# Column tiles 20 to 29 of double blocks 2 to 4: two heads' weights summed over tile pairs, one weight of eight made on ScalarE and GpSimd

## The chip, the cores and the metric

The kernel runs on one core of a Trainium2 chip. The core has five engines that work side by side, each through its own queue in order: TensorE (matmuls; PE in the profile), VectorE (DVE), ScalarE (ACT), GpSimd (POOL) and SyncE (SP, which here only issues DMAs). They wait for one another on semaphores. The metric is the time on the device in microseconds (us). Before the change it is 1262.46 us, the median of three runs (1262.27 to 1264.15).

## The reference

A graph attention layer over 4096 nodes with 256 features and 4 heads, and then a mixture of 8 experts of which each node uses 2:

```python
h = jnp.einsum('nd,hdk->hnk', x, W)                  # x normalised first
s_col = jnp.einsum('hnk,hk->hn', h, a1)
s_row = jnp.einsum('hnk,hk->hn', h, a2)
e = leaky_relu(s_row[:, :, None] + s_col[:, None, :], negative_slope=0.2)
e = jnp.where(adj[None, :, :] > 0, e, NEG_INF)
att = softmax(e, axis=-1)
h_prime = jnp.einsum('hij,hjk->hik', att, h)
y = elu(out) + x @ Wr + br
return gamma * (y - mu) / jnp.sqrt(var + LN_EPS) + beta
...
for e in range(E):                                   # weights w_dense: softmax over the best two
    h = gelu(xf @ W1[e] + b1[e])
    out = out + w_dense[:, e:e + 1] * (h @ W2[e] + b2[e])
```

Both layers are added to their input. The whole 4096 x 4096 attention matrix of each head has to be formed, masked by `adj`, summed and multiplied by `h`.

## The kernel before

**The attention.** The rows (destinations) are worked on in 4 double blocks of 1024 (`a` = 0 to 3 in the code, two halves of 512 each; the text calls them double blocks 1 to 4), and for each of them the kernel walks over 32 column tiles of 128 sources (`j`). The exponential of a leaky relu of a sum is a maximum of two products; factors of a row or of a column alone are taken out of it. What is left is, for each head, `max(er, eb)` with `er` from the row and `eb` from the column, and the mask, which is 0 or 2, takes the rest by a minimum. So one VectorE instruction makes the weights of a head for 128 sources and 1024 rows (`weigh`, L1689, in the order of heads 1, 0, 2, 3). The column's other factor is already in `ha` (the features of the sources) and in `unit` (the same factor, for the sums).

For one tile TensorE then does two things (`attend`, L1212). `rows_of_head` (L1194, matmul L1198) adds weights times features into four accumulator banks `acc`, 16 matmuls; a matmul writes 32 of the array's 128 columns, so that four stand side by side. `weights_of_head` (L1204, matmul L1207) adds weights times `unit` into the bank `den`, from which the sums of the softmax come: 8 matmuls, each with 2 columns that are used. In `den` each head has one quarter, and the halves are its two rows. `queue` (L529) chains every matmul of the loop to the one before it: TensorE's order is the order of the program. In the first and last tile of a double block the sums are done first.

**The masks.** SP loads 512 KB of `adj` for a tile (`load_mask`, L1597), ScalarE turns it into a bfloat16 mask `am` (L1606). There are three buffers of each, and ten of a head's weights (`w`), so VectorE can run at most two and a half tiles ahead of TensorE.

**Finishing a double block.** `finish_blocks` (L1393) is a Python generator: while the loop goes over the next double block, each tile lets it go on by one step (`next(pending, None)`). It divides by the sums, adds the residual, normalises, and then `route_rows` (L1243) chooses the two experts of each row. Its steps at tiles 17 and 18 transpose the rows on TensorE into two banks each (L1253), which ScalarE copies out (L1256); at tile 19 the router's logits take two banks (L1264, copied at L1269), at tiles 20 and 24 one bank each (L1273, L1325). In the end GpSimd writes the rows into the experts' lists with 16 indirect DMAs (L1385), about from tile 25 on.

**PSUM.** There are 8 banks: four are `acc`, one is `den`, and three rotate under the tag "bank" (`bank`, L245) for everything else.

**The order of the other engines.** It isn't written out. The program is handed to a planner, which fixes the order of each engine's queue when the kernel is built: it goes through the work as it becomes ready by its own clock, takes what stands first in the program where several things are ready, and gives a buffer of a tag out when its first instruction is placed. On the chip that order is then kept, whatever comes late.

**Around it.** In double block 4 SP loads the first rows and weights for the experts (`first_tile`, L1580) at tile 3, and TensorE turns those rows after tile 29 (`turn_first`). After it comes the expert phase: 27 jobs of up to 512 rows of one expert, products L1872 and L1906, whose results GpSimd adds into the output (L1931), while the last double block is finished alongside.

Of the kernel before, what the change touches and what calls it, by code (L numbers as in the profile page):

```python
# [18 lines left out]
P = 128  # L19
# [14 lines left out]
LIST = 36 * CH  # L34
PLACE = (2, 3, 0, 1)
ORDER = (1, 0, 2, 3)

# [7 lines left out]
def gat_then_moe(  # L45
# [173 lines left out]
    def forward(apart, stack):  # L219
# [16 lines left out]
        def first_large(name):  # L236
            return fin.tile([P, TB, D], F32, tag="first", name=name, bufs=2)
# [377 lines left out]
        with ExitStack() as layer:  # L615
# [588 lines left out]
            def weights_of_head(w, j, half, h):  # L1204
# [5 lines left out]
                ))  # L1210

            def attend(w, j, halves, sums_first=None):  # L1212

# [21 lines left out]

            def shares_of(pd):

                z = small.tile([P, TB, H, HB], F32, tag="z", name="z")
                for h in range(0, H, 2):
                    nc.vector.reciprocal(z[:, :, h : h + 2], pd[:, :, PLACE[h] : PLACE[h] + 2, :HB])  # L1240
                return z

            def route_rows(b, xe):  # L1243
# [102 lines left out]
                if b == 0:  # L1346
# [34 lines left out]
                    nc.vector.tensor_tensor(others, others, least, OP.max)  # L1381

                for t in range(n):
                    for k in range(2):
# [8 lines left out]
            def finish_blocks(a):  # L1393
# [16 lines left out]
                z = shares_of(pd)  # L1410
                xe = rows_listed()
# [110 lines left out]
            def turn_sums(ud):  # L1522
                pd = bank([P, TB, H, Q], "pd")
                for t in range(TB):
                    queue(nc.tensor.transpose(
                        pd[:, t].rearrange("p h q -> p (h q)"), ud[:, ts(t, P)], ident
                    ))
                z = shares_of(pd)
                return z

# [148 lines left out]
            else:  # L1679

                with tc.tile_pool(name="sep", bufs=2) as work:

                    def weigh(er, am, j, halves):
# [11 lines left out]
                        return w  # L1695

                    both = list(range(HB))
                    ers = [er0, er1]
# [410 lines left out]
```

## Time and profile before

| | |
|---|---|
| time, median of 3 runs | 1262.46 us (1262.27 to 1264.15) |
| the profiled execution | 1260.56 us, span 1258.8 us |
| TensorE's granted clock | 0.999 |
| TensorE busy | 1241.7 us |
| VectorE busy | 845.5 us, of which weights (L1689) 605.9 us, 1275 ns each |
| ScalarE busy | 448.3 us, of which masks (L1606) 130.6 us, 1054 ns each |
| GpSimd busy | 240.4 us |
| matmuls of the attention | L1198 672.1 us in 4096 records, L1207 469.2 us in 2048 |
| double block 3: first matmul of tile 20, of tile 30 | 540.1 us, 592.5 us |

The span runs from the first to the last instruction of the program; the time of an execution has about 2 us around it. Busy times of matmuls overlap, because the ends of pipelined matmuls are modelled: steps from start to start are what counts. In a line of groups stand line, engine, operation, `out<-in`, shape and count, then busy us and mean ns, then the idle time of the engine just before, with what ended it. In a timeline the columns are start, duration, engine, line, operation, and in brackets how long the engine had been idle and what released it.

### The profile page before, as it was taken

What the parts mean: (1) busy time and instruction counts of PE and PEld (TensorE: products, weight loads), DVE (VectorE), ACT (ScalarE), POOL (GpSimd) and SP (SyncE); (2) the same over time, 40 slices, a digit from 0 to 9 for tenths busy, and PEclk for the clock granted to TensorE, in tenths of its full rate; (3) what the DMA queues carried; (4) which work ended last, traced back from release to release, by engine and by line L of the source; (5) the groups of instructions that cost most, each with busy time, mean ns of one, the idle gap of its engine ahead of it and who ended that gap; (6) DMA issues with size and microseconds to landing.
All of it is one profiled execution on the core that took longest, in us unless ns stands there. A gap on an engine that the chain in (4) does not pass through costs nothing.

```text
span 1258.8 us, 22720 instructions
## 1 busy us (share of the span) xinstructions
PE 1241.7 (99%) x8872; PEld 650.4 (52%) x8872; DVE 845.5 (67%) x1566; ACT 448.3 (36%) x918; POOL 240.4 (19%) x217
## 2 busy tenths in 40 slices
PE   9999999999999999999999999999999999999997
PEld 5444444332233332333325324888888876666686
DVE  7998887879999999999999995855111111111120
ACT  4332322265522365322655221533332332222322
POOL 4000000001002601006110024125322222122222
PEclk9999999999999999999999999999999999999999
DMA  6334433536533646334375422868998895455662
GB/s 215 118 118 126 155 107 102 166 104 145 177 114 103 225 112 201 116 94 158 107 178 183 133 70 77 276 171 219 259 236 239 227 219 116 102 139 105 140 160 37
DMA packets 155541, 190.23 MB, mean 151 GB/s; under 512 B 72312, under 2 KB 125680, under 8 KB 155040
## 3 DMA queue, kind: packets, MB, share of 16 engines
q1 hardware_dynamic: 133392, 145.39, 39.7%
q0 software_dynamic: 20544, 36.74, 13.2%
q10 hardware_dynamic: 1488, 6.55, 1.4%
q8 instruction: 71, 1.16, 0.4%
q14 instruction: 46, 0.38, 0.1%
HBM read 155.77 MB, written 29.74 MB: 147 GB/s over the span
## 4 chain that ended last, share of the span: by engine, by line
PE 93%; DVE 3%; issue 1%; ACT 1%; DMA 1%; POOLq 0%; SPq 0%; DVEq 0%; ACTq 0%
PE acc L1198 33%; PE po L1906 18%; PE ph L1872 17%; PE den L1207 17%; PE pr L1053 2%; DVE w L1689 2%; PE ph L1101 2%; PE ptx L1253 0%; DMA early<-lists 0%; PE acc L894 0%; PE pt L780 0%; PE ptr L1491 0%; PE po L1945 0%; PE pl L1264 0%; PE po L875 0%
## 5 line engine op out<-in xcount | busy, mean ns | idle before, releaser
L1198 PE MATMUL acc<-w,ha 128*32 128x512 f32 x4096 | 672.1, 593 | 2.3 <-ACT u L1401 0.9
L1689 DVE SCALAR_TENSOR_TENSOR w<-er,eb,am 128x1024 f32<-128x1024 f32 x496 | 605.9, 1275 | 36.2 <-PE den L1207 30.3
L1207 PE MATMUL den<-w,unit 128*2 128x512 f32 x2048 | 469.2, 592 | 0.4 <-issue 0.3
L1198 PEld LDWEIGHTS acc<-w,ha 128*32 128x32 f32 x4096 | 186.7, 110 | 293.7 <-issue 254.3
L1606 ACT ACTIVATE am<-adj 128x1024 bf16<-128x1024 int32 x124 | 130.6, 1054 | 347.8 <-DVE w L1689 213.1
L1872 PE MATMUL ph<-xT,w 128*128 128x256 f32 (+5 forms) x864 | 230.2, 424 | 2.1 <-issue 1.9
L1906 PE MATMUL po<-w,hT 128*128 128x256 f32 (+1 forms) x1040 | 229.7, 379 | 0.0
L1876 ACT ACTIVATE hT<-ph,bias 128x256 f32<-128x256 f32 (+5 forms) x216 | 111.1, 517 | 290.2 <-issue 185.8
L1906 PEld LDWEIGHTS po<-w,hT 128*128 128x128 f32 (+1 forms) x1040 | 195.7, 189 | 31.2 <-issue 3.1
L1919 DVE SCALAR_TENSOR_TENSOR o<-po,share,b2s 128x256 f32<-128x256 f32 (+2 forms) x66 | 31.7, 482 | 250.2 <-PE po L1906 211.4
L1872 PEld LDWEIGHTS ph<-xT,w 128*128 128x128 f32 x864 | 163.4, 190 | 62.0 <-issue 40.3
L1207 PEld LDWEIGHTS den<-w,unit 128*2 128x2 f32 x2048 | 94.7, 85 | 148.5 <-issue 140.0
L1931 POOL DMA_INDIRECT out<-o,ids x66 | 102.0, 1546 | 321.9 <-DMA out<-o,ids 136.4
L1385 POOL DMA_INDIRECT lists<-xe,at x64 | 88.3, 1379 | 267.6 <-issue 184.7
L1856 DVE STREAM_TRANSPOSE xT<-xr 128x512 f32<-128x512 f32 (+5 forms) x21 | 17.8, 850 | 34.0 <-PE ph L1872 31.2
L1053 PE MATMUL pr<-wr,xT 128*128 128x256 f32 x128 | 30.4, 381 | 0.2 <-ACT er L1147 0.2
L1894 ACT ACTIVATE b2s<-b2b,share 128x256 f32<-128x256 f32 x68 | 30.1, 499 | 0.0
L1121 POOL DMA_DIRECT2D residual<-rb x6 | 4.7, 784 | 121.2 <-DVE rb L1068 121.2
L1441 POOL DMA_DIRECT2D xf<-in_x x6 | 8.1, 1351 | 102.2 <-ACT xf L1440 102.2
L1053 PEld LDWEIGHTS pr<-wr,xT 128*128 128x128 f32 x128 | 24.1, 190 | 5.4 <-issue 0.9
L1101 PE MATMUL ph<-wall,xT 128*128 128x264 f32 x96 | 24.6, 399 | 0.0
L207 ACT ACTIVATE m<-y,off 128x256 f32<-128x256 f32 x48 | 23.7, 495 | 1.1 <-DVE off L215 0.6
(394 smaller groups left out, 618.8 us busy)
## 6 DMA issues: line engine op xcount, KB each, us to landing
adj<-in_adj SPq DMA_DIRECT2D x126, 512.0 KB
w<-in_L_ffn_W SPq DMA_DIRECT2D x54, 1024.0 KB
er<-parts ACTq DMA_DIRECT2D x3, 2048.0 KB
lists<-zeros POOLq DMA_DIRECT2D x8, 520.0 KB
residual<-rb POOLq DMA_DIRECT2D x8, 512.0 KB
rb<-residual SPq DMA_DIRECT2D x8, 512.0 KB
out<-y POOLq DMA_DIRECT2D x8, 512.0 KB
xb<-in_x SPq DMA_DIRECT2D x7, 512.0 KB
```

The lines of the kernel that those rows point to most:

```text
L1053: order_of(nc.tensor.matmul(pr[:, k, :], turned[b][:, c, ts(t0 + k, P)], wr[:, c, :], start=(c == 0), stop=(c == DC - 1),))
L1101: order_of(nc.tensor.matmul(phs[t - t0], xT[:, c, ts(t, P)], wall[:, c, :], start=(c == 0), stop=(c == DC - 1),))
L1198: queue(nc.tensor.matmul(acc[half][h // 2][here : here + Q, :], ha[:, j, h * K + g * Q : h * K + (g + 1) * Q], w[half][h], start=(j == 0), ...
L1207: queue(nc.tensor.matmul(den[here : here + HB, :], unit[:, j, h, 1 - half : 1 - half + HB], w[half][h], start=(j == 0 and half == 0), stop ...
L1385: ins = nc.gpsimd.indirect_dma_start(lists, bass.IndirectOffsetOnAxis(ap=at[:, k, t : t + 1], axis=0), xe[:, t, :], None,).ins
L1606: nc.scalar.activation(am, at, AF.Relu, scale=2.0)
L1689: marks["w"] = nc.vector.scalar_tensor_tensor(wh[:, these], er[:, these, h], eb[:, j, h : h + 1], mask[:, these], op0=OP.max, op1=OP.min,).ins
L1872: order_of(nc.tensor.matmul(ph, job["w1"][:, c, ts(f, P)], xT[:, c, :], start=(c == 0), stop=(c == DC - 1),))
L1876: job["gelu"] = nc.scalar.activation(hT[:, f, :], ph, AF.Gelu, bias=job["bias"][:, f : f + 1]).ins
L1906: order_of(nc.tensor.matmul(po[:size], hT[:, f, k * CH : k * CH + size], w2[:, f, :], start=(f == 0), stop=(f == FC - 1),))
L1919: given_out.append(nc.vector.scalar_tensor_tensor(o[:size], po[:size], share[:size, k : k + 1], b2s[k][:size], op0=OP.mult, op1=OP.add,).ins)
L1931: added.append(add().ins)
```

## The change

It concerns double blocks 2 to 4. In their tiles 20 to 29 (five pairs of an even and an odd tile):

- The sums of heads 1 and 0 are no longer added tile by tile. ScalarE scales the even tile's weights of such a head by the ratio of the two tiles' factors (`ratio`), GpSimd adds the odd tile's weights, and one set of matmuls over the sum serves both tiles (`added_pair`). The ratios are computed at the start of double block 2.
- In the odd tile the weights of head 3 are made without VectorE: ScalarE turns the mask into 0 or 1 (sign), and makes the maximum as a relu of a difference and an addition; GpSimd multiplies by the mask.
- The mask that VectorE reads in these tiles lies in PSUM: ScalarE copies it there, two bfloat16 values as one integer (`packed_mask`). Two tiles of the tag "bank" hold it, taken at tile 20.

In all tiles of double blocks 2 to 4 the quarters of `den` are assigned by head parity and half instead of by head, the matmuls of the sums stand in another order, and the shares are read accordingly. The step of `finish_blocks` that writes the lists waits for tile 30.

```diff
+PAIRED = (20, 30)
+ADDED = (1, 0)
+APART = 3
...
+            def place_of(h, half):
+                return 2 * (h % 2) + half
+            def weights_by_half(w, j, half, h, start=False, stop=False):
+                here = place_of(h, half) * Q
+                queue(nc.tensor.matmul(
+                    den[here : here + HB, :], unit[:, j, h, 1 - h // 2 : 1 - h // 2 + HB],
+                    w[half][h], start=start, stop=stop,
+                ))
+            def attend_both(w, j, alone, summed=None, sums_first=False):
+                halves = range(HB)
+                def first_heads():
+                    for half in halves:
+                        for h in (1, 0):
+                            rows_of_head(w, j, half, h)
+                def other_heads():
+                    if alone:
+                        for h in (1, 0):
+                            for half in halves:
+                                weights_by_half(w, j, half, h, start=(j == 0))
+                    for half in halves:
+                        for h in (2, 3):
+                            rows_of_head(w, j, half, h)
+                    for h in (2, 3):
+                        for half in halves:
+                            weights_by_half(
+                                w, j, half, h, start=(j == 0 and not alone), stop=(j == NT - 1)
+                            )
+                    if summed:
+                        for h in ADDED:
+                            for half in halves:
+                                weights_by_half(summed, j, half, h)
+                parts = (first_heads, other_heads)
+                for add in reversed(parts) if sums_first else parts:
+                    add()
...
+                if not ordered[0]:
+                    yield "lists"
                 for t in range(n):
                     for k in range(2):
                         ins = nc.gpsimd.indirect_dma_start(
...
+                    def packed_mask(am, j):
+                        pm = masks[j % 2]
+                        nc.scalar.copy(pm.bitcast(I32), am.bitcast(I32))
+                        return pm.bitcast(BF16)
+                    def weigh_both(er, a, j):
+                        am = load_mask(a, j)
+                        mask = packed_mask(am, j) if paired(j) else am
+                        w = [[None] * H for half in range(HB)]
+                        for h in ORDER:
+                            wh = work.tile([P, HB, B], F32, tag="w", name="w", bufs=10)
+                            if paired(j) and j % 2 and h == APART:
+                                nc.scalar.sign(am, am)
+                                nc.scalar.activation(
+                                    wh, er[:, :, h], AF.Relu, bias=less[:, j // 2 : j // 2 + 1]
+                                )
+                                nc.scalar.activation(
+                                    wh, wh, AF.Identity, bias=eb[:, j, h : h + 1]
+                                )
+                                nc.gpsimd.tensor_tensor(
+                                    wh, wh, am.rearrange("p (s r) -> p s r", s=HB), OP.mult
+                                )
+                            else:
+                                marks["w"] = nc.vector.scalar_tensor_tensor(
+                                    wh, er[:, :, h], eb[:, j, h : h + 1],
+                                    mask.rearrange("p (s r) -> p s r", s=HB),
+                                    op0=OP.max, op1=OP.min,
+                                ).ins
+                            made[j % 2][h] = wh
...
+                    def added_pair(j):
+                        w = [[None] * H for half in range(HB)]
+                        for h in ADDED:
+                            s = first_large("s").rearrange("p t d -> p (t d)")
+                            s = s.rearrange("p (s r) -> p s r", s=HB)
+                            nc.scalar.activation(
+                                s, made[0][h], AF.Copy, scale=ratio[:, j // 2, h : h + 1]
+                            )
+                            nc.gpsimd.tensor_tensor(s, s, made[1][h], OP.add)
...
                     for a in range(NR):
-                        later = None
+                        later, step = None, None
+                        if a == 1:
...
+                            nc.vector.tensor_scalar(ratio, pairs[:, :, 1], TINY, None, op0=OP.max)
+                            nc.vector.reciprocal(ratio, ratio)
+                            nc.vector.tensor_tensor(ratio, ratio, pairs[:, :, 0], OP.mult)
+                            nc.vector.tensor_scalar(ratio, ratio, 1.0 / EPS, None, op0=OP.min)
...
+                            nc.vector.tensor_scalar(less, alone[:, :, 1], -1.0, None, op0=OP.mult)
                         for j in range(0 if a else TB, NT):
-                            attend(
-                                weigh(er, load_mask(a, j), j, both), j, both,
-                                False if (a, j) == (NR - 1, NT - 1) else None,
-                            )
+                            if a == 0:
+                                attend(weigh(er, load_mask(a, j), j, both), j, both)
+                            else:
+                                if j == PAIRED[0]:
+                                    masks = [bank([P, B], "pm") for k in range(2)]
+                                w = weigh_both(er, a, j)
+                                attend_both(
+                                    w, j, not paired(j),
+                                    added_pair(j) if paired(j) and j % 2 else None,
+                                    j == 0 or j == NT - 1 and a + 1 < NR,
+                                )
                             if a == 0:
                                 prepare_at(TB + j)
-                            if pending:
-                                next(pending, None)
+                            if pending and (step != "lists" or j >= PAIRED[1]):
+                                step = next(pending, None)
```

More of the change, by code (lines that the diff above doesn't have):

```diff
@@ L1234, in attend, with shares_of @@
                     add()
-            def shares_of(pd):
+            def shares_of(pd, by_half):
                 z = small.tile([P, TB, H, HB], F32, tag="z", name="z")
+                if by_half:
+                    for k in range(0, H, 2):
+                        nc.vector.reciprocal(
+                            z[:, :, k : k + 2].rearrange("p t h s -> p t (h s)"), pd[:, :, :, k // 2]
+                        )
+                    return z
                 for h in range(0, H, 2):
@@ L1409, in finish_blocks @@
                     ))
-                z = shares_of(pd)
+                z = shares_of(pd, apart and a > 0)
                 xe = rows_listed()
@@ L1527, in turn_sums @@
                     ))
-                z = shares_of(pd)
-                return z
+                return shares_of(pd, apart)
             def last_block(b, u, z, given, xe):
@@ L1695, in weigh, with paired @@
                         return w
+                    def paired(j):
+                        return PAIRED[0] <= j < PAIRED[1]
+                    def packed_mask(am, j):
[26 more added lines that the diff above has]
+                            made[j % 2][h] = wh
+                            for half in range(HB):
+                                w[half][h] = wh[:, half]
+                        return w
@@ new lines, in added_pair @@
+                    def added_pair(j):
[7 more added lines that the diff above has]
+                            nc.gpsimd.tensor_tensor(s, s, made[1][h], OP.add)
+                            for half in range(HB):
+                                w[half][h] = s[:, half]
+                        return w
@@ L1697, in forward @@
+                    made = [[None] * H for k in range(2)]
+                    ratio = gat.tile([P, NT // 2, 2], F32)
+                    less = gat.tile([P, NT // 2], F32)
                     both = list(range(HB))
@@ L1729, in forward @@
                     for a in range(NR):
[L1730 to L1735 removed]
+                        later, step = None, None
+                        if a == 1:
+                            pairs = unit[:, :, :2, 1].rearrange("p (n k) h -> p n k h", k=2)
+                            nc.vector.tensor_scalar(ratio, pairs[:, :, 1], TINY, None, op0=OP.max)
+                            nc.vector.reciprocal(ratio, ratio)
+                            nc.vector.tensor_tensor(ratio, ratio, pairs[:, :, 0], OP.mult)
+                            nc.vector.tensor_scalar(ratio, ratio, 1.0 / EPS, None, op0=OP.min)
+                            alone = eb[:, :, APART].rearrange("p (n k) -> p n k", k=2)
+                            nc.vector.tensor_scalar(less, alone[:, :, 1], -1.0, None, op0=OP.mult)
+                        for j in range(0 if a else TB, NT):
+                            if a == 0:
[8 more added lines that the diff above has]
+                                    j == 0 or j == NT - 1 and a + 1 < NR,
+                                )
                             if a == 0:
                                 prepare_at(TB + j)
[L1738 to L1739 removed]
+                            if pending and (step != "lists" or j >= PAIRED[1]):
+                                step = next(pending, None)
                             if a == 1 and j == 1:
```

## The prediction

> **What bounds the kernel now.** I read the page's busy line and its chain first, then the timeline of the tiles that the change touches, engine by engine.
>
> ```profile
> PE 1241.7 (99%) x8872; PEld 650.4 (52%) x8872; DVE 845.5 (67%) x1566; ACT 448.3 (36%) x918; POOL 240.4 (19%) x217
> PE 93%; DVE 3%; issue 1%; ACT 1%; DMA 1%; POOLq 0%; SPq 0%; DVEq 0%; ACTq 0%
> 367.30:418.90 51.60, 51.60 (x501) 15.40 (x493) 50.46 (x71) 12.39 (x14) 16.83 (x10) 1.00 0.38 116
> 540.10:591.60 51.50, 51.50 (x491) 15.08 (x483) 49.36 (x64) 12.38 (x14) 16.51 (x11) 1.00 0.40 123
> ```
>
> TensorE is the end of the chain. The last two lines are the windows of tiles 20 to 29 in double blocks 2 and 3 (PE, weight load, DVE, ACT, POOL busy): TensorE is never idle, VectorE nearly full, ScalarE has 12 us of 51, GpSimd 17, all of it list writes.
>
> TensorE's timeline gives the step, VectorE's the rate of the weights:
>
> ```profile
> 353.88 1.09 PE L1253 MATMUL ptx<-ident,xe 128*128 128x128 f32 x8
> 354.90 1.92 PE L1198 MATMUL acc<-w,ha 128*32 128x512 f32 x16
> 356.64 0.60 PE L1207 MATMUL den<-w,unit 128*2 128x512 f32 x2
> 356.66 0.60 PE L1198 MATMUL acc<-w,ha 128*32 128x512 f32 x2
> 357.07 0.60 PE L1207 MATMUL den<-w,unit 128*2 128x512 f32 x2
> 355.43 13.24 DVE L1689 SCALAR_TENSOR_TENSOR w<-er,eb,am 128x1024 f32<-128x1024 f32 x11
> ```
>
> Four recorded matmuls, one for each quarter of the array's columns, start together every 0.43 us. A program matmul is recorded twice (4096 for 2048 in L1198), so four program matmuls cost 0.858 us, and a tile of 24 costs 5.15 us. VectorE makes a weight every 13.24 / 11 = 1.204 us, 4.82 us a tile. It leads, but gains only 0.33 us a tile.
>
> ScalarE's timeline shows what I take to decide the case:
>
> ```profile
> 353.20 1.06 ACT L1606 ACTIVATE am<-adj 128x1024 bf16<-128x1024 int32 x1 [3.73 <-DVE w L1689]
> 357.98 1.06 ACT L1606 ACTIVATE am<-adj 128x1024 bf16<-128x1024 int32 x1 [3.73 <-DVE w L1689]
> 358.94 1.05 ACT L1256 COPY xT<-ptx 128x512 f32<-128x512 f32 x2
> ```
>
> The masks at 353.20 and 357.98 belong to tiles 21 and 22 (counted through L1606). The copies behind them empty the banks that TensorE filled at 353.88, after tile 17: they stand in ScalarE's fixed order behind the mask of tile 22, which waits for VectorE to free a mask buffer, so they come 4 us late. Today this is free: there are three rotating banks and TensorE takes the next.
>
> **What the skill says.** The Trainium skill, "SBUF — State Buffer", Who interferes with whom: a VectorE instruction with two SBUF inputs contends with GpSimd reading SBUF, one with at most one SBUF input outside the 2-port modes does not. GpSimd's timeline agrees with the first half: list writes take 2.08 us while weights are made and 0.97 us once VectorE has stopped. No run here shows the second half.
>
> ```profile
> 751.81 2.08 POOL L1385 DMA_INDIRECT lists<-xe,at  x1 [0.30 <-issue]
> 766.85 0.97 POOL L1385 DMA_INDIRECT lists<-xe,at  x1 [0.30 <-issue]
> ```
>
> "TensorEngine Tiling (Array Packing)", Key Properties: column tiles work independently; the fourfold starts above agree. "PSUM — Partial Sum Buffer", Specifications: a bank holds 512 FP32 values of a partition, so each packed mask fills one.
>
> **The change, part by part.**
>
> *Removed from TensorE.* A pair of tiles has 16 den matmuls. The 8 of heads 1 and 0 become 4 on the summed weights: 4 fewer, 0.858 us. Fifteen pairs (5 in each of 3 double blocks): **-12.87 us**. A pair then takes 10.30 - 0.86 = 9.44 us.
>
> *New order of matmuls, all 96 tiles.* Every four still cover four column quarters, but twice a tile the order within a four turns from quarters 2, 3, 0, 1 to 0, 1, 2, 3 or back. Starts within a four lie about 7 ns apart, so a turn costs 0 to 14 ns: 0 to 2.7 us. I take 0.5.
>
> *VectorE.* Seven weights a pair instead of eight: 7 x 1.204 = 8.43 us, under 9.44. A PSUM input may add some[...]. At worst 7 x 1.28 = 9.0, still under. The set-up at block 2 is five small operations of some 0.16 us (the L177 row, 158 ns), 0.8 us, hidden by VectorE's lead; uncovered, 0.8.
>
> *ScalarE.* Added in a pair: two packs of 512 (L1256's 580 ns), a sign (L1606's 1054), then Relu, Identity and two scaled copies at 1054 plus some 0.09 for a per-partition operand (L1481's 589 against L207's 495): 1.16 + 1.05 + 4 x 1.14 = 6.8 us, and two masks, 2.1: 8.9 us, less about 0.1 overlap per instruction, about 8. Fits 9.44 with little room. Cover gone, it costs its excess over 9.44.
>
> *GpSimd.* A product and two sums of 1024. No such row before: the skill, "GPSIMD Engine Reference", Performance versus the Vector engine, has 4497 ns for 2048, so an estimate of 2.3 us each, 6.9 us a pair, below 9.44. At the port-blocked end (plus 1.2 each) 10.5: over by 1.1 a pair, 16 us in all. The masks in PSUM are there against that, so I take 2.3. The last pair's sums run beside tiles 30 and 31, whose masks are in SBUF: 0 to 1.2 us a block, I take 0.5 in all.
>
> *List writes held to tile 30.* 16 x 2.39 us pitch = 38 us, so they reach some 20 us into the next double block. Behind them on GpSimd: the xf additions (before at 455.63, list writes ended 431.8), now about a microsecond late, used two tiles later; SP's load of the first expert rows at 632.03, with mask loads queued behind it, about equal to the new end; after the last double block they run on in TensorE's expert phase, whose first sum went out at 797.07. Zero; if SP were held, up to 5.
>
> *Two banks.* The packed masks are two tiles of the rotating tag "bank", which has three, from tile 20 to 29. Their first writer is ScalarE, not TensorE with its chained order. Masks of tiles 20 and 21 started at 348.42 and 353.20, before the routing transposes of tile 17 (353.88). If the packs follow their masks, both banks are gone when tiles 17 to 19 want four transposed banks and two of logits. One bank is left, and the second of each couple waits for ScalarE's copy of the first, with all later tiles behind it on TensorE. At tile 17 the copy waits behind the mask of tile 22: 358.94 + 0.57 + 0.1 - (353.88 + 0.44) = 5.3 us; in the other blocks (copies at 531.94 and 705.81, transposes at 526.67 and 700.13) 5.5 and 5.9: **+16.7 us**. By then VectorE has its lead back, so at tiles 18 and 19 only the handing over is paid: transposes drain 0.27, copy 0.58 (0.25 for logits), semaphores 0.1, some 1.5 us a block, up to 2.5 if ScalarE is inside a longer instruction. I take 1.8: **+5.4**. Bounds of the whole: 0 (packs after the transposes) to 25.
>
> Sum on the profiled execution (1260.56: span 1258.8 and 1.8 around it): 1260.56 - 12.87 + 16.7 + 5.4 + 0.5 + 0.5 = 1270.8. The median is 1.9 above that execution: **1272.7**.
>
> **The rivals.**
>
> *A, the forecast (0.54).* The masks take two banks early, TensorE waits for ScalarE. For it: the planner lets ready work go ahead of its place (from 783.11 VectorE mixes the plan's lines 368, 370 and 287 with the first job's 1810, 1823 and 1814), a buffer goes to whoever writes first, and L1606's order shows masks 20, 21 and 22 planned ahead of the routing copies. Own range 1266 to 1281.
>
> *B, the work simply leaves (0.27), the other side.* The packs get their banks only after tile 19's logits. VectorE then loses its lead at tile 20 and remakes it at 1 us a pair: 0 to 1.5 us a block. It decides if pack 20 runs later than about 366 in the old clock. 1262.46 - 12.87 + 1 to 5 = 1251 to 1255. Against it: nothing makes a ready pack wait.
>
> *C, one bank, but copies planned at once (0.19).* The busier ScalarE may be planned with the tile-17 copies ahead of the mask of tile 22: three hand-overs of about 0.9 a block, 8 us, plus 1: 1259, from 1255 to 1263.
>
> A slower GpSimd or ScalarE would come on top of any of them; ScalarE's 8 of 9.44 is why the upper ends are wide.
>
> **How the numbers follow.** A measurement of this kernel tells 0.2%, 2.5 us, from no change. B is faster throughout (0.27), C faster for half of its chance (0.09), the same for 0.08, slower for the rest; A is slower: faster 0.36, same 0.08, slower 0.56. Eight in ten needs most of B as well as A: 1250.5 to 1281; the likeliest case alone is 1266 to 1281.
>
> **What would show it.** The den rows fall by 120 recorded matmuls (15 x 8). Tiles 22 to 28 step by 9.44 us a pair. VectorE's weight rows lose 15; GpSimd gets 45 rows near 2.3 us. Right: in double blocks 2 to 4 TensorE is idle about 5 us inside the tile-17 transposes (released by ScalarE's xT copy), shorter at tiles 18 and 19, packs standing before them on ScalarE. Wrong: no such idle time (B), under 1.5 us at each (C), or a steady shortfall in each pair, with sums waiting for GpSimd.

## The result, and the profile after

| | before | after |
|---|---|---|
| time, median of 4 runs each on the same chip | 1262.37 us (1259.63 to 1264.15) | 1360.38 us (1356.93 to 1361.59) |
| the profiled execution, span | 1258.8 us | 1355.2 us |
| tiles 20 to 29 of double blocks 2, 3, 4 (first matmul of 20 to first of 30) | 53.5, 52.5, 54.6 us | 87.3, 85.3, 85.2 us |
| matmul records | 8872 | 8752 |

The ratio is 1.0774, 95% interval 1.0745 to 1.0803: 98 us slower. The ten tiles lost 257.8 - 160.6 = 97.2 us, and the span grew by 96.4: nearly everything lies there. Tiles 0 to 19 take as long as before to within 1 us, and tiles 17 to 19, with the transposes and the logits, step on in 6.3, 6.3 and 6.1 us in double blocks 2 and 3, before and after.

The page of the kernel after, its busy line and its chain:

```profile
PE 1254.8 (93%) x8752; PEld 651.1 (48%) x8752; DVE 858.4 (63%) x1556; ACT 544.9 (40%) x1023; POOL 327.3 (24%) x262
PE 83%; POOL 8%; issue 3%; ACT 3%; DVE 2%; DMA 0%; POOLq 0%; SPq 0%; DVEq 0%; ACTq 0%
```

TensorE was 93% of the chain and is 83%; GpSimd, which had no share, has 8%. The windows of tiles 20 to 29 in double blocks 2 and 3 (length, then busy PE, weight load, DVE, ACT, POOL, the clock, DMA):

```profile
366.30:453.60 87.30, 59.11 (x477) 15.87 (x470) 59.67 (x69) 44.92 (x49) 53.63 (x31) 0.88 0.27 85
573.90:659.20 85.30, 56.35 (x459) 14.93 (x449) 60.98 (x65) 45.57 (x50) 52.73 (x31) 0.86 0.29 89
```

No engine is full: about 60 us of TensorE and of VectorE, 53 of GpSimd, 45 of ScalarE in 85 to 87. They wait for one another in turn, and TensorE's granted clock, 1.00 in these windows before, is 0.86 to 0.88. TensorE's waits, summed over the program (us, times, longest), name the partner:

```profile
PE acc L1201 <- POOL w L1773: 71.0, 12, 15.1
PE pk L1376 <- DVE on L1371: 6.5, 3, 2.2
PE acc L1201 <- DVE w L1777: 6.4, 3, 2.1
```

71 us go to one operand: head 3's weight of the odd tile, GpSimd's product. GpSimd's timeline in double block 3 shows what stands ahead of it:

```profile
620.68 0.97 POOL L1438 DMA_INDIRECT lists<-xe,at  x1 [0.30 <-issue]
621.68 2.41 POOL L1796 TENSOR_TENSOR s<-s,w 128x1024 f32<-128x1024 f32 x1
624.25 0.99 POOL L1438 DMA_INDIRECT lists<-xe,at  x1 [0.17 <-issue]
625.27 2.35 POOL L1796 TENSOR_TENSOR s<-s,w 128x1024 f32<-128x1024 f32 x1
...
631.63 0.97 POOL L1438 DMA_INDIRECT lists<-xe,at  x1 [0.31 <-issue]
632.63 2.13 POOL L1773 TENSOR_TENSOR w<-w,am 128x1024 f32<-128x1024 f32 x1
...
645.67 2.02 POOL L1438 DMA_INDIRECT lists<-xe,at  x1 [0.31 <-issue]
647.72 4.64 POOL L1796 TENSOR_TENSOR s<-s,w 128x1024 f32<-128x1024 f32 x2
652.31 2.12 POOL L1773 TENSOR_TENSOR w<-w,am 128x1024 f32<-128x1024 f32 x1
```

TensorE's timeline in the same stretch:

```profile
587.82 2.77 PE L1201 MATMUL acc<-w,ha 128*32 128x512 f32 x10 [3.02 <-POOL w L1773]
601.03 1.48 PE L1201 MATMUL acc<-w,ha 128*32 128x512 f32 x10 [2.25 <-POOL w L1773]
634.82 2.77 PE L1201 MATMUL acc<-w,ha 128*32 128x512 f32 x10 [10.89 <-POOL w L1773]
654.49 2.77 PE L1201 MATMUL acc<-w,ha 128*32 128x512 f32 x10 [8.31 <-POOL w L1773]
```

Two things stand in GpSimd's queue ahead of a product. In every pair it is the two sums. In pairs 26/27 and 28/29 it is also the list writes: the planner put all 16 among and ahead of the sums and products. Holding them to tile 30 moved only their place in the program; the planner fills GpSimd's free time with whatever is ready, and they are ready at tile 26 (the first one starts at 618.00, right behind the VectorE step that makes its places).

The clock is a part of the price. The same windows around the wait of 10.89 us:

```profile
628.20:634.80 6.60, 0.00 (x0) 0.00 (x0) 1.42 (x2) 0.00 (x1) 5.62 (x5) 0.50 0.22 81
634.82:638.20 3.38, 3.38 (x16) 0.70 (x18) 0.00 (x0) 1.04 (x1) 2.66 (x3) 0.50 0.50 116
638.30:642.00 3.70, 3.70 (x40) 1.16 (x38) 2.51 (x3) 1.82 (x2) 2.99 (x3) 1.00 0.47 179
```

In the wait the granted clock is one half, and for 3.4 us behind it TensorE still works at half its pace: 16 matmul records in 3.38 us, then 40 in 3.70. By the clock records and the gaps of the trace, TensorE works some 10 us of the ten tiles of each double block like that. That loses about 5 us a block, an estimate of 15 of the 97 us. An even tile that isn't held up still steps on in 4.3 us, five groups of four program matmuls at the full pace of 0.858 us each.

### The profile page after: what moved, and what is told of

Read it like the earlier page. It is cut to its first block, busy times and chain, and to the rows that moved or that the text cites. A ratio compares the mean times of both kernels' runs of the same rounds, so it can differ in the third digit from the quotient of the medians.

```text
span 1355.2 us, 22694 instructions
## 1 busy us (share of the span) xinstructions
PE 1254.8 (93%) x8752; PEld 651.1 (48%) x8752; DVE 858.4 (63%) x1556; ACT 544.9 (40%) x1023; POOL 327.3 (24%) x262
## 3 DMA queue, kind: packets, MB, share of 16 engines
q0 software_dynamic: 20544, 36.74, 12.3%
q8 instruction: 70, 1.15, 0.4%
## 4 chain that ended last, share of the span: by engine, by line
PE 83%; POOL 8%; issue 3%; ACT 3%; DVE 2%; DMA 0%; POOLq 0%; SPq 0%; DVEq 0%; ACTq 0%
PE acc L1201 28%; PE po L2028 17%; PE ph L1994 16%; PE den L1221 10%; PE den L1210 4%; POOL s L1796 3%; POOL lists L1438 3%; PE pr L1056 2%; POOL w L1773 2%; PE ph L1104 2%; DVE w L1777 1%; ACT s L1793 1%; PE ptx L1304 0%; DMA early<-lists 0%; PE acc L897 0%
## 5 line engine op out<-in xcount | busy, mean ns | idle before, releaser
L1201 PE MATMUL acc<-w,ha 128*32 128x512 f32 x4096 | 583.4, 604 | 78.9 <-POOL w L1773 71.0
L1777 DVE SCALAR_TENSOR_TENSOR w<-er,eb,am 128x1024 f32<-128x1024 f32 x264 | 334.6, 1329 | 38.6 <-PE den L1221 27.8
L1201 PEld LDWEIGHTS acc<-w,ha 128*32 128x32 f32 x4096 | 159.5, 111 | 378.1 <-issue 244.2
L1221 PE MATMUL den<-w,unit 128*2 128x512 f32 x1296 | 209.7, 605 | 0.0
L1741 DVE SCALAR_TENSOR_TENSOR w<-er,eb,am 128x1024 f32<-128x1024 f32 x112 | 138.2, 1276 | 13.3 <-PE den L1210 13.3
L1777 DVE SCALAR_TENSOR_TENSOR w<-er,eb,pm 128x1024 f32<-128x1024 f32 x105 | 129.3, 1274 | 24.6 <-ACT pm L1755 24.6
L1796 POOL TENSOR_TENSOR s<-s,w 128x1024 f32<-128x1024 f32 x30 | 71.9, 2408 | 210.4 <-DVE w L1777 176.6
L1210 PE MATMUL den<-w,unit 128*2 128x512 f32 x512 | 117.6, 592 | 0.1
L1221 PEld LDWEIGHTS den<-w,unit 128*2 128x2 f32 x1296 | 44.3, 87 | 101.7 <-issue 96.1
L1438 POOL DMA_INDIRECT lists<-xe,at x64 | 69.9, 1092 | 28.9 <-issue 16.7
L1793 ACT ACTIVATE s<-w,ratio 128x1024 f32<-128x1024 f32 x30 | 33.1, 1142 | 39.5 <-PE den L1221 35.1
L1210 PEld LDWEIGHTS den<-w,unit 128*2 128x2 f32 x512 | 23.5, 85 | 38.8 <-issue 37.7
```

Of the source, the lines that this page charges most:

```text
L1201: queue(nc.tensor.matmul(acc[half][h // 2][here : here + Q, :], ha[:, j, h * K + g * Q : h * K + (g + 1) * Q], w[half][h], start=(j == 0), ...
L1210: queue(nc.tensor.matmul(den[here : here + HB, :], unit[:, j, h, 1 - half : 1 - half + HB], w[half][h], start=(j == 0 and half == 0), stop ...
L1221: queue(nc.tensor.matmul(den[here : here + HB, :], unit[:, j, h, 1 - h // 2 : 1 - h // 2 + HB], w[half][h], start=start, stop=stop,))
L1438: ins = nc.gpsimd.indirect_dma_start(lists, bass.IndirectOffsetOnAxis(ap=at[:, k, t : t + 1], axis=0), xe[:, t, :], None,).ins
L1741: marks["w"] = nc.vector.scalar_tensor_tensor(wh[:, these], er[:, these, h], eb[:, j, h : h + 1], mask[:, these], op0=OP.max, op1=OP.min,).ins
L1777: marks["w"] = nc.vector.scalar_tensor_tensor(wh, er[:, :, h], eb[:, j, h : h + 1], mask.rearrange("p (s r) -> p s r", s=HB), op0=OP.max, ...
```

## The experiments

Each kernel is compared with the kernel before, run beside it on the same chip. The kernel before took 1254.1, 1254.3, 1256.4 and 1254.4 us in the four groups of runs of the experiments, and 1262.4 in that of the change. So kernels of different groups are compared by the second column, or by their ten tiles. Line numbers shift a little with the edits. All results in one table; the tile columns are from the profiled executions, "last" is from the last attention matmul to the end.

| kernel | over before, us | ratio (95%) | tiles 20-29, blocks 2, 3, 4 | last |
|---|---|---|---|---|
| before | | | 53.5, 52.5, 54.6 | 477.6 |
| after | +98.0 | 1.0774 (1.0745 to 1.0803) | 87.3, 85.3, 85.2 | 480.5 |
| order_only | -1.3 | 0.9991 (0.9984 to 0.9997) | 53.5, 52.5, 53.2 | 476.9 |
| lists_behind | +67.9 | 1.0559 (1.0523 to 1.0595) | 74.3, 71.2, 71.4 | 483.8 |
| sums_only | +33.3 | 1.0261 (1.0244 to 1.0278) | 61.2, 58.3, 59.3 | 485.2 |
| apart_only | +14.1 | 1.0108 (1.0091 to 1.0125) | 56.3, 55.2, 56.0 | 482.6 |
| more_s | +46.4 | 1.0363 (1.0346 to 1.0380) | 70.6, 62.7, 64.2 | 484.0 |
| own_first | +40.2 | 1.0316 (1.0298 to 1.0333) | 62.1, 60.9, 63.3 | 485.0 |
| both | +39.7 | 1.0318 (1.0300 to 1.0335) | 62.1, 61.0, 62.5 | 486.0 |
| both_sbuf | +74.3 | 1.0583 (1.0564 to 1.0603) | 74.6, 72.0, 74.5 | 485.2 |
| packs_only | +49.4 | 1.0397 (1.0356 to 1.0438) | 66.9, 67.4, 68.8 | 479.4 |
| packs_spaced | +23.1 | 1.0187 (1.0169 to 1.0204) | 58.1, 55.3, 56.1 | 486.9 |
| first_pairs | +20.2 | 1.0152 (1.0111 to 1.0192) | 58.6, 56.1, 56.7 | 483.0 |
| early_pairs | +53.3 | 1.0419 (1.0383 to 1.0456) | 54.6, 52.5, 53.2 | 478.5 |
| early_sums | +23.7 | 1.0194 (1.0142 to 1.0246) | 53.6, 52.5, 53.2 | 476.9 |

### The parts of the change

**order_only**

```diff
-PAIRED = (20, 30)
+PAIRED = (32, 32)
...
-                if not ordered[0]:
-                    yield "lists"
```

> Only the new assignment of den's quarters and the new order of the matmuls in double blocks 2 to 4 (plus the ratios' set-up), no pairs, no packed masks, no product, lists not held. My prediction's turns: 0 to 2.7 us over before, so 1262 to 1265. If the order or the set-up costs more than argued: over 1267.

Measured 1252.79 us, 0.9991: neither the new order nor the ratios' set-up costs anything.

**lists_behind**

```diff
+                with ExitStack() as held:
+                    for name in ("product", "sum"):
+                        if name in marks:
+                            held.enter_context(tc.issue_after(marks[name]))
                     for t in range(n):
                         for k in range(2):
                             ins = nc.gpsimd.indirect_dma_start(
```

`marks` holds the last sum and product; `issue_after` fixes the order in GpSimd's queue and adds no wait.

> The changed kernel, with one thing altered: each double block's 16 list writes stand in GpSimd's queue behind the last sum and the last product of that double block. Theory L (the list writes, which the planner set among and ahead of the sums and products of pairs 26/27 and 28/29, cost about 18.5 us a block: in the changed kernel the steps from tile 27 to 28 and from 29 to 30 add up to 33.7 to 34.9 us, the pairs without list writes pay 7.6 for such a step): 1360 - 56 = about 1304 us, between 1296 and 1312, and the steps 27-28 and 29-30 near 8 us. Theory R (the lists only fill time in which GpSimd waits for ScalarE anyway; the pair's own chain of scaled copy, sums, product sets the time): 1340 us or more, with the same long steps.

Measured 1321.98, 67.9 over before: 30 us less than the change, between the two theories. The ten tiles gave back 257.8 - 216.9 = 40.9 us; of the 11 us between these two numbers, 8 come from the slower kernel before in the change's own group, and 3.3 from the last part, below. The steps from tile 27 to 28 are 9.4, 7.2, 7.2 us (17.7 to 23.5 in the changed kernel), as theory L said; those from 29 to 30 only fall from 10.4 to 17.2 us to 10.1 to 12.7. There the last pair's work now runs beside VectorE's first weights with masks in SBUF:

```profile
618.98 5.70 POOL L1800 TENSOR_TENSOR s<-s,w 128x1024 f32<-128x1024 f32 x2 [5.01 <-ACT s L1797]
624.64 3.10 POOL L1777 TENSOR_TENSOR w<-w,am 128x1024 f32<-128x1024 f32 x1
```

(5.70 for 4.73 us, 3.10 for 2.13.) That is 1.9 us of it; the rest isn't assigned. And 3.3 us came back in the last part: there the list writes end later, and with them the load of the next expert rows from the lists. The timeline of VectorE in a later kernel with the same place of the list writes (both) shows the wait:

```profile
822.49 0.17 DVE L1954 CAST ids<-early 128x2 int32<-128x2 f32 x1 [8.38 <-DMA early<-lists]
...
823.03 0.36 DVE L1286 RECIPROCAL z<-pd 128x16 f32<-128x16 f32 x2
```

The reciprocals stand behind that cast on VectorE, and TensorE's next bank behind the reciprocals: 7.7 us there.

So theory L has the larger part of what was expected, and a second cause, worth more, was left. That is what the next two were for.

**sums_only**

```diff
-                            if paired(j) and j % 2 and h == APART:
+                            if False:
```

(on top of lists_behind)

> The changed kernel with list writes behind, and without the weight made apart: VectorE makes all eight weights of a pair, GpSimd has the two sums alone. Theory Q (what is left over after the lists is the product standing behind the two sums of its own pair in GpSimd's queue): TensorE waits for no product, only VectorE is tight (8 x 1.2 to 1.27 = 9.6 to 10.2 us a pair): 1250 to 1268, I say 1258. If the sums by themselves are late (scaled copies waiting for their two buffers, 4.7 us of GpSimd): over 1280.

Measured 1287.4, +33.3: a miss by 21 us. TensorE waits for no sum in these tiles; it waits for VectorE's weights (8.9 us in 11 waits), and follows VectorE's pace, 52.5 us of work in the 58.3 us of double block 3. I had priced VectorE by its weights alone (9.6 us a pair) and left out the routing steps (2.7 us in order_only's double block 3: 50.9 us busy, 40 x 1.204 = 48.2 of them weights), its lost lead at tile 20, and the last part's delay (485.2 against 476.9).

**apart_only**

```diff
-                                    w, j, not paired(j),
-                                    added_pair(j) if paired(j) and j % 2 else None,
+                                    w, j, True, None,
```

(on top of lists_behind)

> The changed kernel with list writes behind, and without the sums: all den matmuls stay, one weight of eight is made by ScalarE and GpSimd. Theory Q: the product has GpSimd to itself and comes in time; TensorE's pair stays at 10.30 us: 1260 to 1268, I say 1263. If the chain sign, relu, addition, product is too slow by itself: over 1280.

Measured 1268.24, +14.1, 5 us of it in the last part. TensorE never waits for the product here: the chain sign, relu, addition, product is quick enough when nothing stands ahead of it. Together in lists_behind the two parts cost 67.9, alone 33.3 and 14.1: the rest, 20.5 us or more (both hold the packed masks), is how they stand to each other.

### The two parts against each other

**more_s**

```diff
-                            s = first_large("s").rearrange("p t d -> p (t d)")
+                            s = (large if j % 4 == 1 else first_large)("s")
+                            s = s.rearrange("p t d -> p (t d)")
```

(on top of lists_behind, as own_first is)

> As lists_behind, with the scaled copies and sums of every second pair in three other, idle buffers (tag large), so that a pair's copies need not wait for the matmuls of the pair before. Theory S (the two buffers close a ring: den matmuls of one pair, scaled copies, 4.7 us of sums, product, head 3 of the next odd tile; in lists_behind ScalarE waits 2.6 to 4.0 us a pair for those matmuls and TensorE then 1.8 to 4.1 us a pair for the product): TensorE's waits for the product, 31.9 us, go below 10; 20 to 30 us faster than lists_behind, so 38 to 48 us over the kernel before. Theory P (only the product's place behind the sums matters, since the sums wait for the odd tile's weights anyway): within 8 us of lists_behind, 60 to 76 us over before.

Measured 1300.71: 21 us better than lists_behind, theory S's 20 to 30. TensorE's waits for the product:

```profile
PE acc L1201 <- POOL w L1777: 13.3, 9, 3.3
PE pk L1376 <- DVE on L1371: 11.3, 3, 3.8
```

from 31.9 us, not quite to the 10 expected.

**own_first**

```diff
-                                nc.scalar.activation(
+                                marks["apart"] = nc.scalar.activation(
                                     wh, wh, AF.Identity, bias=eb[:, j, h : h + 1]
-                                )
+                                ).ins
...
+                            with tc.issue_after(marks["apart"]):
                                 nc.scalar.activation(
                                     s, made[0][h], AF.Copy, scale=ratio[:, j // 2, h : h + 1]
                                 )
+                            with tc.issue_after(marks["product"]):
+                                marks["sum"] = nc.gpsimd.tensor_tensor(
+                                    s, s, made[1][h], OP.add
+                                ).ins
```

> As lists_behind, with the order inside a pair turned on two queues: ScalarE makes relu and addition of head 3 ahead of the two scaled copies, GpSimd the product ahead of the two sums. Theory P: TensorE waits for no product; the sums are needed only by the last four matmuls of the pair, and 4.7 us of GpSimd fits; 25 to 35 us faster than lists_behind, 33 to 43 us over before, what is left being VectorE's (the idle time at tile 20, its routing steps). Theory S (the ring over the two buffers sets the pace whatever the order): within 10 us of lists_behind, with waits of TensorE for sums in place of those for products.

Measured 1294.52: 27 us better than lists_behind, theory P's 25 to 35. The waits moved to the sums, as theory S had named, but are half as long:

```profile
PE den L1221 <- POOL s L1802: 14.5, 12, 2.3
...
PE acc L1201 <- POOL w L1777: 3.2, 3, 1.1
```

Some 13 us of the gain are the clock. With these shorter waits it is 0.99 to 1.00 over the ten tiles, in lists_behind 0.93 to 0.94; by the same estimate, half pace costs 14 us in lists_behind and 1 us here.

**both**

> own_first and more_s together: no ring and no product behind sums. If these two were all of GpSimd's part in the loss: TensorE waits for GpSimd below 3 us, and 25 to 35 us over before is left, all of it VectorE's (about 1.8 us at tile 21, and pairs of 10 to 11 us where routing steps stand between the weights). If GpSimd's and ScalarE's work on a pair is too much in itself (6.9 and 8.9 us of 9.44): 45 us or more over before, waits for GpSimd remaining.

Measured 1293.95, +39.7; with the product first the other buffers add nothing (0.6 us). So the ring and the queue are one cause: it runs through the product's place behind the sums, and either cut opens most of it, the turned order more (with the other buffers alone 13.3 us of waits for the product are left). The 14.5 us of waits for sums remain (the last one, 2.25 us in double block 3, is the pair beside the masks in SBUF), with VectorE's lead and the last part (+8.4 us): the time lies between the two cases, and waits for GpSimd remain, as in the second.

A part of VectorE's delay that I had not counted is seen in lists_behind: the same routing step, twice, on VectorE.

```profile
583.74 2.19 DVE L1348 TENSOR_TENSOR oh<-oh,first 128x64 f32<-128x64 f32 x1
...
595.42 0.21 DVE L1348 TENSOR_TENSOR oh<-oh,first 128x64 f32<-128x64 f32 x1
```

The first ran beside a sum of GpSimd (581.11 to 585.84) and took 2.19 us, the second alone 0.21.

**both_sbuf**

```diff
-                        mask = packed_mask(am, j) if paired(j) else am
+                        mask = am
...
-                                if j == PAIRED[0]:
-                                    masks = [bank([P, B], "pm") for k in range(2)]
```

(on top of both)

> As both, with no packed masks: VectorE reads the bfloat16 mask in SBUF in all tiles, no banks are taken, no packs made. Theory C (a weight with two SBUF inputs and a GpSimd instruction shut each other out, as the routing steps with SBUF inputs show, 0.21 us alone and 2.2 us beside a sum): 6.9 us a pair of GpSimd on top of 8.4 of VectorE, 15.3 against 10 to 11 us a pair, so 60 to 75 us slower than both. Theory V (the contention is mild and what the banks cost is VectorE's lead: it is idle 5.4 us at tile 20 for the first pack and 4.7 us more for the logits): 10 to 25 us faster than both.

Measured 1328.56, 34.6 over both. Theory V fell, though VectorE does keep its lead (tile 20 to 21 takes 4.77 us, in both 6.35). Theory C has the direction, with half its size: a pair's two sums take 6.6 us instead of 4.7 and single weights up to 3.39 instead of 1.27, but not the full sum of both engines. The masks in PSUM earn their place.

### What the packed masks and the list writes do

**packs_only**

```diff
+PACKED = (20, 30)
...
-                        return PAIRED[0] <= j < PAIRED[1]
+                        return False
...
-                        mask = packed_mask(am, j) if paired(j) else am
+                        mask = packed_mask(am, j) if PACKED[0] <= j < PACKED[1] else am
```

(and the list writes not held)

> Only the new order and the packed masks of tiles 20 to 29 in two PSUM banks; no sums, no weight made apart, lists not held, TensorE's work as before. My prediction's step on the two banks put this at +22.1 us (waits inside the transposes of tiles 17 to 19). The traces of the changed kernel show no such wait; what they show is that the packs wait for banks and VectorE loses its lead (idle 5.4 us at tile 20 and 4.7 us behind the logits). Theory V: TensorE pays about 1.8 us at tile 21, and then follows VectorE, which has 48.2 to 49 us of weights and 2.3 of routing steps for 52.5: 3 to 12 us over before in the three blocks, 4 to 10 likeliest. The prediction's step: 16 us or more, before tile 20. If the packs cost nothing: under 2.5 us.

Measured 1305.73, +49.4, more than any theory had and in another place. Up to tile 27 it goes as theory V says (7.2 and 6.2 us at the first two steps, for 5.6 and 5.2 in order_only). Then one tile takes 13.9, 16.1 and 16.8 us. TensorE's timeline there:

```profile
598.75 1.03 PE L1222 MATMUL den<-w,unit 128*2 128x512 f32 x5
600.02 1.03 PE L1222 MATMUL den<-w,unit 128*2 128x512 f32 x3 [0.23 <-issue]
...
605.00 1.02 PE L1202 MATMUL acc<-w,ha 128*32 128x512 f32 x2 [1.08 <-issue]
606.41 4.09 PE L1202 MATMUL acc<-w,ha 128*32 128x512 f32 x6 [0.40 <-issue]
611.32 1.31 PE L1222 MATMUL den<-w,unit 128*2 128x512 f32 x3 [0.81 <-issue]
614.14 0.62 PE L1222 MATMUL den<-w,unit 128*2 128x512 f32 x3 [1.51 <-issue]
```

TensorE waits for no engine ("issue") and starts a few instructions every 0.70 us. The clock is not the reason: it is 1.00 from 598.70 to 614.10. GpSimd's timeline shows list writes at full pace:

```profile
599.25 0.97 POOL L1437 DMA_INDIRECT lists<-xe,at  x1 [0.30 <-DMA lists<-xe,at]
600.53 0.97 POOL L1437 DMA_INDIRECT lists<-xe,at  x1 [0.31 <-issue]
601.80 0.97 POOL L1437 DMA_INDIRECT lists<-xe,at  x1 [0.30 <-issue]
```

Sixteen follow at 1.27 us from 591.50; after six or seven TensorE slows down, and it recovers at 614.2, when the packets of the last one have landed. With masks in SBUF they go at up to 2.39 us, because VectorE's weights hold them up.

**packs_spaced**

```diff
+                        with tc.issue_after(ins):
+                            gap = nc.gpsimd.memset(idle, 0.0).ins
```

(after each list write of packs_only, and the next one behind it)

> As packs_only, with a GpSimd memset of an idle 128x1024 tile (about 1 us) behind each list write, so that the writes follow one another every 2.3 us instead of every 1.27. Theory D (in packs_only TensorE is starved in tiles 27 to 29 because sixteen list writes run at full pace, no longer slowed by VectorE's reads; its matmuls then start 0.70 us apart with nothing to wait for but issue, until the last write's packets have landed): the 14 to 16 us at tiles 27 to 29 go away and the packs' own cost is left, 2.7 us a block: 8 to 14 us over before, tiles 20 to 30 in 55 to 57 us. Theory M (TensorE is slow because VectorE reads masks from PSUM, whatever the list writes do): 40 us or more over before, with the same starvation.

Measured 1277.49, +23.1. The slow stretch is gone: no tile from 27 to 29 takes over 6.8 us. Theory M falls; the pace of the list writes is the cause. The ten tiles cost 4.6, 2.8 and 2.9 us over order_only, together 10.3: this is what the packed masks themselves cost. Of the rest, 10 us are in the last part and of my own making: with the memsets between them half the writes now fell beside VectorE's weights for tile 30 and later, whose masks are in SBUF, and there one of them took 23.39 us, and one in double block 4 10.22. GpSimd's timeline in double block 3:

```profile
596.90 23.39 POOL L1442 DMA_INDIRECT lists<-xe,at  x1 [0.17 <-issue]
```

VectorE in the same stretch:

```profile
596.64 22.80 DVE L1784 SCALAR_TENSOR_TENSOR w<-er,eb,am 128x1024 f32<-128x1024 f32 x19
```

Nineteen weights with two operands in SBUF, without a gap: the write ended right after the last of them. Density alone doesn't explain it: in the kernel before, writes beside weights just as dense took 1.0 to 2.1 us (2.08 at 751.81). Why this one was held for so long stays open. The writes end late, and the expert phase with them (last part 486.9).

### Another place for the pairs

All three have own_first's order (early_sums without the weight made apart), and the list writes as before the change.

**first_pairs** (`PAIRED = (20, 24)`)

> own_first's order with pairs only in tiles 20 to 23 (2 of 5), list writes in their former place, free of sums and products around them. Saves 6 x 0.858 = 5.1 us of TensorE. Theory: without the list writes and with the product first, what remains is the loss at the pack of tile 20 (1.5 to 1.8 us a block) and the late sums of two pairs (0.8 to 1.1 each): 0 to 6 us over before. If above 12 us, the pairs lose by themselves even there.

Measured 1276.62, +20.2: a miss. The tiles cost 3.6 to 5.1 us a block over order_only, 12.3 in all, twice the upper end of what was expected: so even here the pairs and their packed masks lose by themselves. And I had not reckoned with what follows: in double block 4 the last list write starts 11.2 us after tile 30 instead of 7.0, and the last part is 6 us longer (TensorE waits 5.1 us for ScalarE in the expert phase). What links these isn't settled.

**early_pairs** (`PAIRED = (6, 16)`)

> own_first's order with the pairs in tiles 6 to 15 instead of 20 to 29 and the list writes in their former place: no list writes near, no transposed banks in use, VectorE with its full lead and 1 to 2 us of other steps. TensorE saves 12.9 us. If the loss at tiles 20 to 29 was of that place (list writes, banks, routing steps): 12 us faster to 2 us slower than before. But ScalarE has 2 to 7 us a pair of the finishing of the block before on top of the pair's 8.9 of 9.44: if that binds, 10 to 40 us slower, with TensorE waiting for products and sums behind ScalarE.

Measured 1309.64, +53.3, 50 of it in the first twenty tiles of the three blocks. The second half of the expectation holds in its direction, but its 40 us are exceeded; in its cause it holds only partly. GpSimd's queue in double block 2 has DMAs of the block before ahead of a product:

```profile
311.01 0.86 POOL L1501 DMA_DIRECT2D y<-xf  x1 [1.43 <-DVE y L1500]
314.33 0.81 POOL L1511 DMA_DIRECT2D out<-y  x1 [2.46 <-ACT s L1792]
315.15 2.15 POOL L1771 TENSOR_TENSOR w<-w,am 128x1024 f32<-128x1024 f32 x1
```

and TensorE waits 4.34 us for that product.

**early_sums**

> As early_pairs without the weight made apart: VectorE makes all eight weights. ScalarE has 5.5 us a pair and the finishing, which fits; VectorE needs 8 x 1.2 = 9.6 us and 0.1 to 1 of other steps for TensorE's 9.44, and begins with a lead of two and a half tiles: 9 us faster to 5 us slower than before; I say 3 faster. Over 12 slower would mean that GpSimd's sums, behind its DMAs of the finishing, are what is late.

Measured 1280.04, +23.7: the "over 12" case in number, but not in cause. In the trace, taken of a run 8 us below the median, TensorE waits 7.4 us for VectorE's weights and 3.2 for sums; the rest is not assigned. No version was found that beats the kernel before by more than the 0.1% of order_only.

## Why the prediction was wrong

Slower was right, but by luck: the wait that made the forecast slower does not occur, and two others, which it had put at nothing, do. 1272.7 us was wrong: 1360.38 lies far outside 1250.5 to 1281. By its own steps:

- **Removed from TensorE, -12.87 us**: right as a size. The records fall by 120, and an even tile not held up, with five groups of four matmuls instead of six, steps on in 4.3 us.
- **New order, 0 to 2.7 us**: 0 (order_only).
- **Durations**: right. The sums take 2408 ns and the product 2196 for the estimate of 2.3 us, ScalarE's copies 1142, packs 580, relu 1.14, addition 1.15; VectorE's weights with masks in PSUM 1274, for 1275 in the kernel before.
- **Two banks, +16.7 and +5.4 us**: the mechanism fell. ScalarE's timeline after, in double block 3, is the answer to the one I built it on:

```profile
563.87 1.06 ACT L1658 ACTIVATE am<-adj 128x1024 bf16<-128x1024 int32 x1 [3.73 <-DVE w L1777]
564.84 1.05 ACT L1307 COPY xT<-ptx 128x512 f32<-128x512 f32 x2
567.47 1.07 ACT L1307 COPY xT<-ptx 128x512 f32<-128x512 f32 x2 [1.58 <-PE ptx L1304]
568.58 0.59 ACT L1755 COPY pm<-am 128x512 int32<-128x512 int32 x1
```

  The first pack comes after the copies of tile 18's transposes, the second, at 577.31, after the logits of tile 19: the planner gave the banks to TensorE's work and let the packs wait. That is rival B's order in the main. What it costs is VectorE's lead (idle 5.41 us before the first weight of tile 20 and 4.67 before the logits), and B had that too small: 0 to 1.5 us a block, measured 2.8 to 4.6 (packs_spaced).
- **"GpSimd 6.9 us a pair, below 9.44" and "ScalarE about 8, fits"**: the step that failed first, an overlap taken for granted. As sums they fit; as a chain they don't. I compared the work of a pair with the time of a pair and did not ask in which order the two queues do it. The product, needed in the middle of the odd tile, stood behind the two sums, needed only at its end; the sums waited for scaled copies, and these for their two buffers, which the den matmuls of the pair before release. Turning the order is worth 27 us (own_first), cutting the ring 21 (more_s).
- **List writes held to tile 30, zero**: the step that failed most plainly. They weren't held, and standing ahead of sums and products they cost 40.9 us in the ten tiles (lists_behind). I had written that the planner lets ready work go ahead of its place, used it against the packs, and not asked the same of the list writes. Even where they are held back, the cover I named is gone at the end of double block 4: the load of the expert rows comes late.
- **Masks in PSUM against a slower GpSimd**: right (both_sbuf is 34.6 us slower). The routing steps were left out, which have both operands in SBUF and stretch from 0.2 to over 2 us beside a sum.
- **VectorE, 8.43 us a pair**: right for the weights, but in tiles 20 to 29 it had 50.46 us of 51.60 in a view that I showed myself. Without its lead, every routing step and every pack is paid.
- **TensorE's pace behind a wait**: taken as full throughout. Long waits bring the half clock with them, about 15 us in the ten tiles (the estimate above), which is inside the terms below.

The sum as the runs give it, in the ten tiles of three blocks, over order_only (159.2 us): the list writes in GpSimd's queue 40.9; the order inside the pairs 216.9 - 186.4 = 30.5 (own_first), of which some 13 are the clock; what is left, 27.2, holds the packed masks' 10.3 and is for the rest late sums and VectorE's pace. All that against the 12.87 saved, which the 27.2 already has in it. I did not separate that rest further, nor how much of the 40.9 is TensorE slowed by the pace of the list writes rather than the queue.

## What to carry to other kernels

When work goes to an engine that has slack, compare its latency with the moment when each result is needed, in the order of that engine's queue, and not only its busy time with the period; put first what is needed first. Where a planner makes the order, moving a step in the program does not hold it back: it goes as soon as its inputs are ready, so order it behind something on its own engine, and then look for who waits for its output. A lead of one engine over another is a resource: a step that makes it wait once, like a first pack, is paid for as long as that engine has no slack to catch up.

## What the runs showed of the hardware that was not expected

- A dense row of indirect list writes slows TensorE: after six or seven at 1.27 us each (0.97 and 0.30), its instructions come a few at a time every 0.70 us, with no engine to wait for, until the packets have landed; 9 to 13 us of the ten tiles in each double block (packs_only against packs_spaced), where writes 2.1 us apart cost nothing of the kind. The kernel before seems to have it too at its end: in double block 4 ten writes start 1.27 to 1.41 us apart, and tiles 30 and 31 start 7.3 and 7.9 us after their predecessors (5.9 and 5.2 in order_only). What is held up isn't shown. Instructions that are fetched late are an unlikely cause: in packs_only no DMA packet of the kind "instruction" starts between 592.0 and 615.9, and TensorE recovers at 614.2 without one.
- TensorE's granted clock falls to one half in long waits and stays there for 3.4 to 4.2 us of work behind them (634.82 to 638.25 and 654.49 to 658.73 in the kernel after). Where the longest waits are 2.1 to 2.3 us (sums_only, both), it is 1.00 over the ten tiles.
- The Trainium skill, "SBUF — State Buffer", Who interferes with whom, says that a VectorE instruction with two SBUF inputs contends with a GpSimd instruction that reads SBUF, and that one with at most one SBUF input, outside the 2-port modes, doesn't contend with GpSimd. Both halves are now seen: list writes take 0.97 to 1.03 us beside masks in PSUM (double block 3 of packs_only) and 0.97 to 2.1 beside masks in SBUF (before). What I had not expected is how far it goes both ways: a routing step of 0.21 us took 2.19 beside a sum, and one list write took 23.39 us beside nineteen weights without a gap.
